# Layer two's contexts as whole blocks in six PSUM banks for blocks 0 to 12, with scale, offset and residual in slots of their own

## The chip, the cores and the metric

The kernel runs on one core of a Trainium2 chip. The metric is the device time in microseconds (us); the time before is the median of three runs. TensorE (PE) multiplies, VectorE (DVE), ScalarE (ACT) and GpSimd (POOL) work elementwise, and SyncE (SP) issues the DMAs.

## What is computed

`x` has 128 graphs of 64 nodes with 768 features, and each graph has a 64 x 64 adjacency. Everything is 32-bit floating point. Cut to what matters:

```python
h = jnp.maximum(_layernorm(x, axis=-1), 0.0)
for l in range(2):
    m_left  = jnp.einsum('bsh,oh->bso', h, W_left[l])
    m_right = jnp.einsum('bsh,oh->bso', h, W_right[l])
    u_left  = jnp.einsum('bih,bjh->bij', h, m_left) / temper
    u_right = jnp.einsum('bih,bjh->bij', h, m_right) / temper
    u = u_left * adj_tri + u_left * diag_mask + u_right * jnp.swapaxes(adj_tri, 1, 2)
    delta_exp_u = jnp.exp(u) * adj
    attention = delta_exp_u / (jnp.sum(delta_exp_u, axis=2, keepdims=True) + 1e-10)
    h_lin = jnp.einsum('bsh,oh->bso', h, W_lin[l]) + b_lin[l]
    ctx = jnp.matmul(attention, h_lin)
    h = jax.nn.relu(_layer_norm(ctx, ln_a[l], ln_b[l]))
return x + h
```

`_layer_norm` subtracts the mean over the 768 features, divides by the standard deviation (with `ddof=1`) plus 1e-3, multiplies by `ln_a` and adds `ln_b`. For layer two the last lines become: scale each row of the context by one number and by the row `a`, add the row `b` (the offset), take the maximum with zero and add `x` (the residual).

## The kernel before

The 8192 tokens are cut into 16 blocks (`NB`) of 512 tokens, that is 8 graphs. Each layer has two passes over them. `pass_one` makes the scores and the attention and stores it in DRAM. `pass_two` makes `h_lin` and the context of each block and finishes its rows. The change lies in layer two's `pass_two`, where `last` is true.

**The projection.** `linear(u, ...)` makes `h_lin` of block `u` from 15 products (`ORDER`), numbered 0 to 14: sums of token chunks times sums of weight chunks. The products go to four PSUM banks, X, Z, Y and V, in the order X Z X Y X V X Y X V X Y V Z V. After each product `read` adds the bank into the tile `hl`: the first time that a part of `hl` is written by ScalarE (`L305`), later ones by VectorE (`L223`). Four times per block a bank is begun anew with a bias in it: `fresh` lets ScalarE copy it there (`L843`, "preload") ahead of the product. The preload of V for product 9 is issued after product 6; it has to wait until the V of product 5 has been read.

**The token sums.** Eleven of the products use sums of token chunks (`T_SUMS`), made by GpSimd (`L223`, tile `ts`) a block ahead, from slot 15 on. Ahead of them ScalarE applies layer one's affine and relu to the loaded tokens (`affine`, `L382`, six parts from slot 9).

**Slots.** The order of the work on each engine is that of issue. `put(slot, f)` files a function; `linear` runs slot `2*i` in the middle of product `i`, after its first two matmul calls, and slot `2*i+1` after the product and its reads. What is filed at 30 or later is moved to the next block (30 becomes 0). Every engine's queue is in order, so a slot is a place in the queues and not a time: an instruction that waits holds what is queued behind it on its engine.

**The context in two halves.** A block has four tiles of 128 rows, numbered (r, k). `finish(u, r)` calls `context` for the two tiles of half `r`: 8 calls of 64 x 64 tiles on 384 columns into four banks (`aux0`, `aux1`). ScalarE squares both tiles with a sum along the row and takes the root (`L1022`, `L1024`), VectorE makes the inverse (`L1027`, `L1028`). For layer two, `scaled` then lets VectorE multiply each tile by its inverse and by `a` in one instruction (`L1032`) and GpSimd add `b` (`L1035`, the offset). `done` lets VectorE take the maximum with zero and add `x` in one instruction (`L1046`, the residual), and SP store the rows (`L1048`). `residual` loads `x` into the tiles `xr` (`L962`), of which there are four. In layer two every block `u - 1` is finished so within `linear(u)`: half 0 after product 0, half 1 after product 7, with slots 6, 7, 8, 11, 12 and 20, 21, 22, 30, 30 for inverse, two scalings and two residuals.

**The context in one.** Layer one's blocks 0 to 12 are finished by `finish_block(u - 1)` after product 12 of `linear(u)`. `context_block` makes all four tiles in one group of 16 calls, on 512 and 256 columns, into six banks: those of `aux0` and `aux1` used more tightly, and X and Y of the projection. VectorE copies the parts in X and Y to SBUF (`L972`), after which X gets its preload for the next block. ScalarE squares eight pieces (`squares`, `L983`, slots 25, 26, 28, 29); the deviation and inverse follow in slots 30 and 32, and the scaling of the pieces in slots 33 to 36. In layer one this scaling is ScalarE's (`L997`), with no `a`, offset or residual: layer two applies those to the tokens as it loads them.

Of the kernel before, what the change touches and what calls it, by code (L numbers as in the profile page):

```python
# [13 lines left out]
ALU = mybir.AluOpType  # L14
# [3 lines left out]
def kernel(  # L18
# [12 lines left out]
    nc = tc.nc  # L31
# [33 lines left out]
    def put(slot, *fs):  # L65
        plan.setdefault(slot, []).extend(fs)
# [780 lines left out]
    def pass_two(l, aside):  # L847
        last = l == L - 1
        with (tc.tile_pool(name=f"ps_two{l}", bufs=1, space=bass.MemoryType.PSUM) as ps,
# [108 lines left out]
            def residual(u, r):  # L958
                XS[u, r] = [sp.tile([P, H], F32, name="xr", bufs=4) for _ in range(2)]
                for k in range(2):  # L960
                    for h in range(PAIR):
                        nc.sync.dma_start(XS[u, r][k][h * S:(h + 1) * S], x[u * NBB + batch(r, k, h)])  # L962

            def finish_block(u, more):

                parts = context_block(u)
                tiles = ((0, 0), (0, 1), (1, 0), (1, 1))
                zs = {t: sp.tile([P, H], F32, name="z", bufs=4) for t in tiles}
                cut = (slice(0, T), slice(T, H))

                for t in ((1, 1), (1, 0)):
                    nc.vector.tensor_copy(zs[t][:, cut[0]], parts[t][0])  # L972
                    parts[t][0] = zs[t][:, cut[0]]
                    if t == (1, 1):
                        AHEAD.append(fresh(l, 0, more))
                ss = stat.tile([P, Q, 2], F32, name="ssb", bufs=2)
                sd = stat.tile([P, Q], F32, name="sdb", bufs=2)
                rs = stat.tile([P, Q], F32, name="rsb", bufs=2)

                def squares(t):  # L980
                    junk = zs[0, t[1]]
                    for n in range(2):
                        nc.scalar.activation(junk[:, cut[n]], parts[t][n], AF.Square,  # L983
                                             accum_out=ss[:, 2 * t[0] + t[1], n:n + 1])

                def deviation():
                    nc.vector.reduce_sum(sd, ss, axis=mybir.AxisListType.X)
                    nc.scalar.activation(sd, sd, AF.Sqrt, bias=floor, scale=1.0 / (H - 1.0))

                def inverse():  # L990
                    nc.vector.tensor_scalar_add(rs, sd, EPS_LN)
                    nc.vector.reciprocal(rs, rs)

                def scaled(t):
                    by = rs[:, 2 * t[0] + t[1]:2 * t[0] + t[1] + 1]
                    for n in range(2):
                        nc.scalar.activation(zs[t][:, cut[n]], parts[t][n], AF.Copy, scale=by)  # L997
                    kept(u, *t, zs[t])

                order = ((1, 1), (1, 0), (0, 0), (0, 1))  # L1000
                for f, slots in ((squares, (25, 26, 28, 29)), (scaled, (33, 34, 35, 36))):
                    for n, t in zip(slots, order):
                        put(n, lambda f=f, t=t: f(t))
                put(30, deviation)
                put(32, inverse)

            def kept(u, r, k, z):
                for h in range(PAIR):
# [2 lines left out]
            def finish(u, r):  # L1011

                cx = context(u, r)
                zs = [sp.tile([P, H], F32, name="z", bufs=4) for _ in range(2)]
                if last and not u and not r:
                    residual(u, r)
                two = "p (n d) -> p n d"
                ss = stat.tile([P, 2], F32, name="ss", bufs=2)
                sd = stat.tile([P, 2], F32, name="sd1", bufs=2)
                rs = stat.tile([P, 2], F32, name="rs1", bufs=2)  # L1020
                for k in range(2):
                    nc.scalar.activation(zs[k].rearrange(two, n=2), cx[k], AF.Square, accum_out=ss[:, k:k + 1])  # L1022

                nc.scalar.activation(sd, ss, AF.Sqrt, bias=floor, scale=1.0 / (H - 1.0))  # L1024

                def inverse():
                    nc.vector.tensor_scalar_add(rs, sd, EPS_LN)  # L1027
                    nc.vector.reciprocal(rs, rs)  # L1028

                def scaled(k):  # L1030
                    if last:
                        nc.vector.scalar_tensor_tensor(  # L1032
                            zs[k].rearrange(two, n=2), cx[k], rs[:, k:k + 1],
                            rows["a"].rearrange(two, n=2), op0=ALU.mult, op1=ALU.mult)
                        nc.gpsimd.tensor_add(zs[k], zs[k], rows["b"])  # L1035
                        return
                    if (u, r, k) == (NB - 1, 1, 1):
                        nc.vector.tensor_scalar_mul(zs[k].rearrange(two, n=2), cx[k], rs[:, k:k + 1])
                    else:
                        nc.scalar.activation(zs[k].rearrange(two, n=2), cx[k], AF.Copy, scale=rs[:, k:k + 1])  # L1040
                    kept(u, r, k, zs[k])

                def done(k):
                    if last:
                        xs = XS[u, r]
                        nc.vector.scalar_tensor_tensor(xs[k], zs[k], 0.0, xs[k], op0=ALU.max, op1=ALU.add)  # L1046
                        for h in range(PAIR):
                            nc.sync.dma_start(out[u * NBB + batch(r, k, h)], xs[k][h * S:(h + 1) * S])  # L1048
                        if k and u + r < NB - 1 and (u, r) != (NB - 2, 0):
                            residual(u + r, 1 - r)  # L1050

                steps = [lambda f=f, k=k: f(k) for f in (scaled, done) for k in range(2)]
                return [inverse] + (steps if last else steps[:2])

# [37 lines left out]
            for u in range(NB):  # L1092
                turn = not last and u >= NB - 2
                put(4, lambda u=u: load_at(u))
                if u + 1 < NB:
                    if u:
                        load_h(2, l, u + 1)
                        put_all(9, affine(2, l, u + 1))
                    put_sums_t((2, l, u + 1), 15 if u else 21, 1, 0)
                    if not last and NB - 5 <= u < NB - 3:  # L1100
                        load_rows(1, u + 5 - NB, sp)
                        put_all(14, transpose_rows(1, u + 5 - NB, sp), 2)
                    if not last and u >= NB - 3:
                        put(2, lambda u=u: load_h(1, 1, u + 3 - NB))
                        put_all(21 if u == NB - 3 else 11, affine(1, 1, u + 3 - NB), 1 if u == NB - 3 else 3)
                    if u in aside:
                        aside[u]()
                    ends = {}
                    if u and last:
                        ends = {0: ((u - 1, 0), (6, 7, 8, 11, 12)), 7: ((u - 1, 1), (20, 21, 22, 30, 30))}  # L1110
                    elif u > NB - 3:
                        ends = {5: ((u - 1, 0), (16, 17, 18)), 11: ((u - 1, 1), (28, 29, 30))}
                    elif u:
                        ends = {12: (u - 1, None)}
                    linear(u, (0, 1), 0, ends, (0, 1) if u + 2 < NB else (0,))
                    for n in sorted(plan):
                        plan[n - 30] = plan.pop(n)
                else:
                    if turn:
                        put_token_ops(1, 0, "before")  # L1120
                        assert not idle, len(idle)
                        for n in range(RINGS - 1):
                            put(20 + 4 * n, lambda n=n: stream(1, n))
                        ends = ({1: ((u - 1, 0), (13, 14, 16)), 11: ((u - 1, 1), (34, 35, 36))},
                                {4: ((u, 0), (50, 51, 52))})
                    else:
                        last_block(u)
                        put(8, lambda: residual(u - 1, 1))
                        ends = ({0: ((u - 1, 0), (12, 13, 15, 19, 31)), 9: ((u - 1, 1), (28, 29, 30, 39, 41))},
                                {2: ((u, 0), (44, 48, 51, 61, 62))})  # L1130
                    linear(u, (0,), 0, ends[0], (1,))
                    linear(u, (1,), 30, ends[1], ())
                    for n in sorted(plan):
                        run(n)
                    for f in (finish_last if last else finish)(u, 1):
                        f()
# [72 lines left out]
```

## Time and profile before

| what | value |
|---|---|
| median of three runs | 2706.51 us (2705.50 to 2709.24) |
| profiled execution: own time, span | 2705.84 us, 2704.1 us |
| granted TensorE clock | 0.998 |
| busy: PE, DVE, ACT, POOL | 2677.7, 1499.1, 832.4, 1381.4 us |
| layer one's second pass, whole blocks | about 941 to 1304 us of the span |
| layer two's second pass | about 2226 us to the end |
| VectorE scaling `L1032` | 62 of 1.01 us |
| GpSimd offset `L1035` | 62, 1.82 us median |
| VectorE residual `L1046` on `xr` | 60, 2.02 us median, 0.95 to 2.44 |

A line of the profile names engine, code line, operation, tiles (written `out<-in`), shapes, a count and durations. "L1046" is line 1046 of the kernel. Several instructions of one kind in a row are merged on the timeline: the first number is the start and the second the time until the last one ends. In brackets stands how long the engine was idle before, and what released it. The product names are those of the banks, so "V" is a product, or a read, in bank V.

### The profile page before, as it was taken

Reading aid. Unit: us, or ns where it says so; the run is one execution under the profiler, and the core shown is the slowest. Engines: PE = TensorE matmul, PEld = TensorE weight load, DVE = VectorE, ACT = ScalarE, POOL = GpSimd, SP = SyncE. Lnnn points to the kernel's source line nnn. Section 1 sums busy time; section 2 is a strip of 40 time slices with the busy share of each in tenths; the row PEclk is TensorE's granted clock in tenths of the full one; section 3 lists DMA queues with packets and bytes.
Section 4 is the critical chain, followed back from the end, with each engine's and each line's share of the span. In section 5 each row is a group of like instructions: output and inputs, shape, how many; then the busy total and the mean of one; then the engine's idle time right before and its main releaser. Section 6 shows DMA issues by size and latency. Waiting matters only on the chain.

```text
span 2704.1 us, 47306 instructions
## 1 busy us (share of the span) xinstructions
PE 2677.7 (99%) x18514; PEld 2301.3 (85%) x18514; DVE 1499.1 (55%) x2456; ACT 832.4 (31%) x1617; POOL 1381.4 (51%) x1071
## 2 busy tenths in 40 slices
PE   9999999999999999999999999999999999999998
PEld 8788888888888888888788888888888888888886
DVE  7664755756647433334344545546446475666667
ACT  4032131221310254454631221221212304445443
POOL 6633244333336765566433325335244286887886
PEclk9999999999999999999999999999999999999999
DMA  8886956858765345558594956968759524655655
GB/s 272 268 309 212 289 197 208 279 202 265 244 207 181 102 143 184 166 167 255 184 284 174 317 187 212 286 191 279 229 193 301 211 79 135 182 160 159 186 154 148
DMA packets 310222, 567.81 MB, mean 210 GB/s; under 512 B 62832, under 2 KB 190064, under 8 KB 301808
## 3 DMA queue, kind: packets, MB, share of 16 engines
q1 hardware_dynamic: 309840, 564.39, 64.9%
q8 instruction: 148, 2.42, 0.4%
q14 instruction: 74, 0.61, 0.1%
q10 hardware_dynamic: 160, 0.39, 0.0%
HBM read 429.40 MB, written 135.27 MB: 209 GB/s over the span
## 4 chain that ended last, share of the span: by engine, by line
PE 96%; DVE 1%; SPq 0%; issue 0%; DMA 0%; ACT 0%; DVEq 0%; ACTq 0%
PE right L535 17%; PE X L1069 12%; PE X L535 11%; PE V L535 11%; PE Z L535 9%; PE Y L535 9%; PE V L1069 8%; PE Y L1069 6%; PE both L474 5%; PE Z L1069 4%; PE aux L877 2%; PE aux L900 1%; PE Y L900 0%; PE Z L474 0%; DVE wp L223 0%
## 5 line engine op out<-in xcount | busy, mean ns | idle before, releaser
L223 POOL TENSOR_TENSOR ts<-ht 128x512 f32<-128x512 f32 x352 | 481.6, 1374 | 172.6 <-PE X L1069 69.6
L223 POOL TENSOR_TENSOR ts<-ht,ts 128x512 f32<-128x512 f32 x192 | 252.9, 1324 | 345.7 <-PE V L535 202.1
L535 PE MATMUL right<-ts,wp 128*128 128x252 f32 (+1 forms) x1632 | 380.9, 376 | 0.6 <-DVE wp L223 0.6
L535 PEld LDWEIGHTS right<-ts,wp 128*128 128x128 f32 x1632 | 310.0, 190 | 39.5 <-DVE wp L223 1.0
L483 POOL TENSOR_TENSOR wm<-adj,tri 128x256 f32<-128x256 f32 x60 | 42.3, 728 | 490.7 <-DMA wp<-ws 274.5
L223 DVE TENSOR_TENSOR m<-m,X 128x512 f32<-128x512 f32 x160 | 105.5, 684 | 257.9 <-ACT m L305 180.2
L223 DVE TENSOR_TENSOR m<-m,right 128x504 f32<-128x504 f32 (+1 forms) x304 | 199.5, 674 | 87.8 <-PE right L535 74.1
L1069 PE MATMUL X<-room,ts 128*128 128x256 f32 x1024 | 244.0, 380 | 0.2
L535 PE MATMUL Z<-ts,wp 128*128 128x256 f32 x992 | 234.3, 379 | 0.0
L223 POOL TENSOR_TENSOR ts<-ht,ht 128x512 f32<-128x512 f32 x128 | 163.2, 1285 | 137.8 <-PE right L535 92.8
L1069 PEld LDWEIGHTS X<-room,ts 128*128 128x128 f32 x1024 | 191.7, 190 | 31.7 <-issue 1.8
L535 PEld LDWEIGHTS Z<-ts,wp 128*128 128x128 f32 x992 | 188.4, 190 | 24.9
L535 PE MATMUL X<-ts,wp 128*128 128x256 f32 x872 | 207.5, 381 | 1.9 <-DVE wp L223 1.9
L535 PE MATMUL V<-ts,wp 128*128 128x252 f32 (+1 forms) x864 | 201.6, 376 | 0.0
L305 ACT ACTIVATE m<-right 128x504 f32<-128x504 f32 (+1 forms) x64 | 36.2, 592 | 506.8 <-PE both L474 486.8
L535 PEld LDWEIGHTS X<-ts,wp 128*128 128x128 f32 x872 | 164.4, 190 | 25.5 <-POOL ts L223 2.3
L382 ACT ACTIVATE ht<-ht,b_col,a_col 128x512 f32<-128x512 f32 x192 | 141.3, 806 | 140.9 <-DMA ht<-h 140.9
L1069 PE MATMUL Y<-room,ts 128*128 128x256 f32 x768 | 182.5, 379 | 0.0
L535 PEld LDWEIGHTS V<-ts,wp 128*128 128x128 f32 x864 | 164.2, 190 | 20.4
L1069 PEld LDWEIGHTS Y<-room,ts 128*128 128x128 f32 x768 | 145.8, 190 | 20.4 <-issue 0.6
L223 DVE TENSOR_TENSOR hl<-hl,V 128x512 f32<-128x512 f32 (+1 forms) x136 | 89.2, 656 | 128.9 <-PE V L1069 118.7
L223 DVE TENSOR_TENSOR m<-m,Y 128x512 f32<-128x512 f32 x144 | 95.8, 684 | 116.0 <-PE Y L535 105.2
(225 smaller groups left out, 4866.3 us busy)
## 6 DMA issues: line engine op xcount, KB each, us to landing
wp<-ws SPq DMA_DIRECT2D x435, 512.0 KB, 6.3
ht<-h SPq DMA_DIRECT2D x62, 1536.0 KB, 8.3
h<-room SPq DMA_DIRECT2D x112, 384.0 KB, 7.1
z<-z SPq DMA_DIRECT2D x128, 192.0 KB, 3.1
ws<-wp SPq DMA_DIRECT2D x93, 256.0 KB, 4.2
xr<-in_x_dram SPq DMA_DIRECT2D x120, 192.0 KB, 3.6
out_dram<-xr SPq DMA_DIRECT2D x120, 192.0 KB, 2.6
room<-z SPq DMA_DIRECT2D x112, 192.0 KB, 5.1
```

The costliest lines, as they stand in the source:

```text
L223: (eng.tensor_add if sign == "+" else eng.tensor_sub)(o, a, b)
L305: nc.scalar.activation(to(o), p, AF.Copy, scale=1.0 if sign == "+" else -1.0)
L382: nc.scalar.activation(ht, ht, AF.Relu, bias=cols[1][:, c:c + 1], scale=cols[0][:, c:c + 1])
L474: nc.tensor.matmul(p[h * S + e:h * S + e + 32, q, e:e + 95], ht[:, c, b * S + e:b * S + e + 32], mb[:, e:e + 95], start=(c == 0), stop=(c ...
L483: nc.gpsimd.tensor_tensor(wm[:, :, k], adj[:, :, 1 - k], tri[:, k].unsqueeze(1).to_broadcast([P, Q, S]), op=ALU.mult)
L535: nc.tensor.matmul(p[:, g], wk[:, c, g * P:(g + 1) * P], tk[:, c, :].rearrange("p (b s) -> p b s", s=S)[:, :, :ns], start=(new and g == c ...
L877: nc.tensor.matmul(cx[k][i, m, :HH], at[j, q, :], hl[j, q, m * HH:(m + 1) * HH], start=True, stop=True)
L900: nc.tensor.matmul(parts[r, k][n][i], at[j, q, :], hl[j, q, cut], start=True, stop=True)
L1069: nc.tensor.matmul(p[:, n], b[t][:, c, r * P:(r + 1) * P], w[s][:, c, :], start=(i in FIRST and i not in PRELOAD and n == c == 0), stop=(c ...
```

## The change

- In layer two, blocks 0 to 12 go through `finish_block` as in layer one. The copy of tile (1, 0) out of Y is then ScalarE's instead of VectorE's.
- The scaling is done in place of `L1032` by two VectorE instructions per tile, one for each piece; the offset stays GpSimd's. Both are in slots 33 to 36, so 3 to 6 of the block after.
- The residual has slots 38 to 41, so 8 to 11, for the tiles (1,1), (1,0), (0,0) and (0,1); it is moved to a function, `added_rows`.
- The `x` rows of a block are loaded in slot 12, all eight loads together, those of block 0 in slot 20 of `linear(0)`.
- The last three blocks keep their halves; the halves of block 13 now follow products 6 and 11 of `linear(14)`, and those of block 14 products 2 and 10 of `linear(15)`, with later slots.

```diff
--- before.py
+++ after.py
@@ -969,7 +969,7 @@
                 cut = (slice(0, T), slice(T, H))
 
                 for t in ((1, 1), (1, 0)):
-                    nc.vector.tensor_copy(zs[t][:, cut[0]], parts[t][0])
+                    (nc.scalar.copy if last and t == (1, 0) else nc.vector.tensor_copy)(zs[t][:, cut[0]], parts[t][0])
                     parts[t][0] = zs[t][:, cut[0]]
                     if t == (1, 1):
                         AHEAD.append(fresh(l, 0, more))
@@ -993,17 +993,34 @@
 
                 def scaled(t):
                     by = rs[:, 2 * t[0] + t[1]:2 * t[0] + t[1] + 1]
+                    if last:
+                        for n in range(2):
+                            nc.vector.scalar_tensor_tensor(zs[t][:, cut[n]], parts[t][n], by, rows["a"][:, cut[n]],
+                                                           op0=ALU.mult, op1=ALU.mult)
+                        nc.gpsimd.tensor_add(zs[t], zs[t], rows["b"])
+                        return
                     for n in range(2):
                         nc.scalar.activation(zs[t][:, cut[n]], parts[t][n], AF.Copy, scale=by)
                     kept(u, *t, zs[t])
 
                 order = ((1, 1), (1, 0), (0, 0), (0, 1))
-                for f, slots in ((squares, (25, 26, 28, 29)), (scaled, (33, 34, 35, 36))):
+                steps = [(squares, (25, 26, 28, 29)), (scaled, (33, 34, 35, 36))]
+                if last:
+                    steps.append((lambda t: added_rows(u, *t, zs[t]), (38, 39, 40, 41)))
+                    for r in range(2):
+                        put(42, lambda r=r: residual(u + 1, r))
+                for f, slots in steps:
                     for n, t in zip(slots, order):
                         put(n, lambda f=f, t=t: f(t))
                 put(30, deviation)
                 put(32, inverse)
 
+            def added_rows(u, r, k, z):
+                xs = XS[u, r][k]
+                nc.vector.scalar_tensor_tensor(xs, z, 0.0, xs, op0=ALU.max, op1=ALU.add)
+                for h in range(PAIR):
+                    nc.sync.dma_start(out[u * NBB + batch(r, k, h)], xs[h * S:(h + 1) * S])
+
             def kept(u, r, k, z):
                 for h in range(PAIR):
                     nc.sync.dma_start(ROWS[u][batch(r, k, h)], z[h * S:(h + 1) * S])
@@ -1012,8 +1029,6 @@
 
                 cx = context(u, r)
                 zs = [sp.tile([P, H], F32, name="z", bufs=4) for _ in range(2)]
-                if last and not u and not r:
-                    residual(u, r)
                 two = "p (n d) -> p n d"
                 ss = stat.tile([P, 2], F32, name="ss", bufs=2)
                 sd = stat.tile([P, 2], F32, name="sd1", bufs=2)
@@ -1042,12 +1057,9 @@
 
                 def done(k):
                     if last:
-                        xs = XS[u, r]
-                        nc.vector.scalar_tensor_tensor(xs[k], zs[k], 0.0, xs[k], op0=ALU.max, op1=ALU.add)
-                        for h in range(PAIR):
-                            nc.sync.dma_start(out[u * NBB + batch(r, k, h)], xs[k][h * S:(h + 1) * S])
-                        if k and u + r < NB - 1 and (u, r) != (NB - 2, 0):
-                            residual(u + r, 1 - r)
+                        added_rows(u, r, k, zs[k])
+                        if k and (u, r) == (NB - 3, 1):
+                            residual(NB - 2, 0)
 
                 steps = [lambda f=f, k=k: f(k) for f in (scaled, done) for k in range(2)]
                 return [inverse] + (steps if last else steps[:2])
@@ -1106,8 +1118,11 @@
                     if u in aside:
                         aside[u]()
                     ends = {}
-                    if u and last:
-                        ends = {0: ((u - 1, 0), (6, 7, 8, 11, 12)), 7: ((u - 1, 1), (20, 21, 22, 30, 30))}
+                    if last and not u:
+                        for r in range(2):
+                            put(20, lambda r=r: residual(0, r))
+                    if last and u > NB - 3:
+                        ends = {6: ((u - 1, 0), (18, 19, 20, 23, 24)), 11: ((u - 1, 1), (28, 29, 30, 33, 34))}
                     elif u > NB - 3:
                         ends = {5: ((u - 1, 0), (16, 17, 18)), 11: ((u - 1, 1), (28, 29, 30))}
                     elif u:
@@ -1126,7 +1141,7 @@
                     else:
                         last_block(u)
                         put(8, lambda: residual(u - 1, 1))
-                        ends = ({0: ((u - 1, 0), (12, 13, 15, 19, 31)), 9: ((u - 1, 1), (28, 29, 30, 39, 41))},
+                        ends = ({2: ((u - 1, 0), (14, 15, 17, 21, 31)), 10: ((u - 1, 1), (29, 30, 31, 39, 41))},
                                 {2: ((u, 0), (44, 48, 51, 61, 62))})
                     linear(u, (0,), 0, ends[0], (1,))
                     linear(u, (1,), 30, ends[1], ())
```

## The prediction

> **What bounds the kernel now.** I read the page first (shares and chain), then the busy table of the steady stretches of both second passes, then the timelines of one block each. All times are of the one profiled execution.
>
> ```profile
> PE 2677.7 (99%) x18514; PEld 2301.3 (85%) x18514; DVE 1499.1 (55%) x2456; ACT 832.4 (31%) x1617; POOL 1381.4 (51%) x1071
> ...
> PE 96%; DVE 1%; SPq 0%; issue 0%; DMA 0%; ACT 0%; DVEq 0%; ACTq 0%
> ```
>
> TensorE is the bound and has no slack. A microsecond gained elsewhere is worth nothing; a wait put in front of a matmul is paid in full. Layer one's second pass already uses six banks for whole blocks, so its blocks price the new form. One block of each layer, in the busy table of the two stretches:
>
> ```profile
> core 0: us, PE busy (x) PEld busy (x) DVE busy (x) ACT busy (x) POOL busy (x), PEclk, DMA share, GB/s
> 1001.37:1030.21 28.84, 28.84 (x153) 23.75 (x153) 10.82 (x17) 13.49 (x36) 18.78 (x16) 1.00 0.48 160
> 2341.50:2370.70 29.20, 29.20 (x153) 23.60 (x153) 19.86 (x25) 13.68 (x26) 23.64 (x16) 1.00 0.57 167
> ```
>
> Layer one repeats every 28.84 us and layer two every 29.20 us, both with TensorE full. The fifteen projections cost the same (1.727 us each); what differs is the contexts, 2.94 us in one group against 3.30 in two. But layer two has 9 us more VectorE work and 5 us more GpSimd work per block, the part that the change rearranges. The next views show what those do to each other, first before (VectorE, then GpSimd):
>
> ```profile
> 2350.43 0.69 DVE L223 TENSOR_TENSOR hl<-hl,V 128x512 f32<-128x512 f32 x1 [0.91 <-PE V L1069]
> 2351.04 3.99 DVE L1046 SCALAR_TENSOR_TENSOR xr<-z,xr 128x768 f32<-128x768 f32 x2
> 2357.26 1.28 DVE L223 TENSOR_TENSOR hl<-hl,X 128x512 f32<-128x512 f32 x2 [2.23 <-PE X L1069]
> ...
> 2348.68 3.60 POOL L1035 TENSOR_TENSOR z<-z,b 128x768 f32<-128x768 f32 x2 [3.78 <-DVE z L1032]
> 2352.23 3.93 POOL L223 TENSOR_TENSOR ts<-ht 128x512 f32<-128x512 f32 x2
> 2356.24 1.27 POOL L223 TENSOR_TENSOR ts<-ts,ht 128x512 f32<-128x512 f32 x1
> ```
>
> The residual instruction (L1046, both inputs in SBUF) takes 2.0 us here and 0.95 where GpSimd is idle (the two at 2691.4). GpSimd's sum takes 1.97 beside it and 1.27 alone. Read one by one, the first L1046 ends 0.82 us after the offset addition L1035 ends, and the next sum can only then begin: the two engines take turns. So in steady overlap a residual costs 0.82 behind whatever GpSimd holds, and GpSimd waits for it. Today two residuals form a batch and sit after the V read (the first line), so the delay reaches no matmul.
>
> **What the Trainium skill says.** "SBUF — State Buffer", section "Who interferes with whom": a VectorE instruction with two SBUF inputs contends with a GpSimd instruction that reads SBUF, and one with at most one SBUF input does not. The trace agrees: L1046 is slowed to 2.02 (median), L1032 with its PSUM input stays at 1.01 in all 62 cases. Section "SBUF: two separate sides": whichever starts first has the port for its whole instruction; the trace's turns agree. "TensorE: Matmul & The Clock Gate", section "Why this matters for your kernels", warns of idle gaps over about 3 us; the granted clock here is 1.00 and no such gap occurs in these stretches, so no run here shows it. I take no clock loss for gaps of 2 us.
>
> **The change part by part.** I set 0 at the start of product 0 of a block. The layer-one timeline gives TensorE's places (block from 1004.86):
>
> ```profile
> 1013.49 1.89 PE L1069 MATMUL V<-room,ht 128*128 128x256 f32 x8
> ...
> 1018.67 1.89 PE L1069 MATMUL X<-room,ht 128*128 128x256 f32 x8
> 1020.40 1.89 PE L1069 MATMUL V<-room,ht 128*128 128x256 f32 x8
> 1022.12 1.89 PE L1069 MATMUL X<-room,ts 128*128 128x256 f32 x8
> ...
> 1017.64 0.59 ACT L843 COPY V<-bias 128x512 f32<-128x512 f32 x1
> ```
>
> Product 5 (V) ends at 10.4; product 9 starts bank V anew at 15.54, and needs before it VectorE's read of product 5 (0.69) and ScalarE's preload (0.59). So that read must start by about 14.2. Product 10 writes X at 17.26, and needs VectorE's two reads of product 8 (1.28), which must start by 15.9.
>
> *Contexts.* Two groups become one: 3.30 − 2.94 = 0.36 us of TensorE saved in each of 13 blocks, −4.6 us. The banks X and Y are asked for at 22.5; their last reads are done by about 21.6 in layer one, and the preload of X for the next block ends 3.8 us before its use (1029.87 against 1033.7). Both hold here: nothing else of VectorE lies there. The copy moved to ScalarE (0.6) delays the squares, which end near 0.6 instead of 0.06, and their reduction waits anyway for V's read at 0.8. ScalarE's next read is due at 1.9. Eight square pieces replace four, about as in layer one; hidden. No cost, unless VectorE is late there.
>
> *Scaling, slots 3 to 6.* Eight pieces instead of four whole rows. VectorE gets to them after the Z read, at 4.9 (layer one: 1009.75). By width from 0.87 a piece-pitch for 768 in SBUF, 0.92 from PSUM, 0.61 and 0.34 for 512 and 256 reads: each tile 0.95, together 3.8. So they end at 8.7, and the Y read of product 3 runs to 9.3 (Y is written at 12.1; no loss).
>
> *Offset, same slots.* Four L1035 of 1.77 pitch on GpSimd, queued one after the other instead of two and two. The first becomes ready at 6.0, but the SBUF half of the second tile's scaling holds the port to 6.5. It runs 6.5–8.3, the second 8.3–10.0.
>
> *Residual, slots 8 to 11.* Three of the four now stand in VectorE's queue ahead of product 5's V read. They take turns with the offsets: residual 1 waits to 10.0, ends 10.9; offset 3 to 12.6; residual 2 to 13.4; offset 4 to 15.2; residual 3 to 16.0. V's read runs 16.0–16.6, the preload to 17.25, and product 9 starts at about 17.3: **1.8 us late**. The fourth residual then waits for the first transform sum (1.2 us of port) and ends at 18.05. The X reads of product 8 end at 19.3, and product 10, now free from 19.0, waits another 0.3. Sum: **2.0 us per block**. ScalarE stands behind the preload too (two affine parts and Y's read of product 7), but these are done by 19.3, ahead of the Y product at 21.
>
> The rest of the block is in time: the sums start at 16 and end at 30.7 of a 30.8 us block (11 × 1.27), each ahead of its use.
>
> *DMAs.* Per block still 8 stores, 8 residual loads, one token load and one attention load, all on SP. The stores follow the residuals to 18.6; the loads at slot 12 wait for those stores to land (2.6 to 3.4 us) and go out from about 19 to 25 (0.6 each); then the next token load, landing (8.3 us) some 3 into the next block, where the affine parts want it at 8.6. No cost; if SP were 5 us later, the affine parts would be late next.
>
> *Count.* The stall comes in blocks 2 to 13 in full: 12 × 2.0 = 24.0. In block 14 half a context stands ahead of product 9 (1.64 us), so little is left; its squares wait for z tiles, its residual loads land about 25 into it: +0.7 for this and the moved ends of block 15, bounds −1 and +3. Block 0's loads at slot 20 and the last two blocks' other halves are neutral. Total: −4.6 + 24.0 + 0.7 = +20.1; I take **+20**. Against the profiled execution (span 2704.1, own time 2705.84) that is 2725.9; against the median 2706.51, 0.7 above it, **2726.5**.
>
> Not shown by the trace: who wins the port when both wait, with four offsets in a row. If GpSimd always does, as in the 13 repetitions seen, the stall is 2.0 (1.5 to 2.4 for errors in the start and the piece widths). If the port cost nothing at all, the offsets would end at 7.8, 9.6, 11.3 and 13.1, residual 3 at 12.2, the V read would be in time and the stall 0. These are the two ends.
>
> **Rivals.**
>
> *A, the turns with the offsets delay the V read:* +20, own range +13 to +26.
>
> *B, VectorE sometimes wins twice:* residuals 1 and 2 go together at 10.0, residual 3 follows offset 3 at 13.4, the V read is in time at 14.2–14.9, and only the fourth residual, behind offset 4, holds the X reads (to 18.2, 0.9 late). 12 × 0.9 − 4.6 + 0.7 = +7, 2713. Against it: no L1046 in the trace goes ahead of a waiting GpSimd instruction.
>
> *C, no stall:* the V read starts before 14.2, because the offsets begin or proceed faster than I queue them; it decides there. Then only the contexts count: −4.6, 2701.9, not slower. For it: VectorE has 9 us free per block, and layer one runs this form at 28.84. Against it: layer one's scaling is on ScalarE and has no offset or residual.
>
> *D, a longer chain:* the fourth residual or late loads push the reads of products 10 and 11 too, or delay the token load; another 1 to 2 us per block, +32 to +44. Against it: the margins above.
>
> That the change does nothing for TensorE is not likely: the same function gives 28.84 in layer one.
>
> **Chances and range.** A 0.65, B 0.12, C 0.15, D 0.08. A measurement of this kernel tells about 0.2% (5.4 us) from no change. A and D are slower, B mostly (0.09); C, at 0.17%, is mostly within (0.11), and 0.04 of it beyond. So slower 0.82, same 0.14, faster 0.04. The range from 2708 to 2742 holds A, most of B and the near part of D; it leaves out C.
>
> **What would show it.** Right: TensorE idle once per block in layer two ahead of product 9's V (about 1.8 us, behind ScalarE's preload, itself behind VectorE), and a trace of it ahead of product 10; a block of about 30.8 us; offsets of 1.8 alternating with residuals of over 2 us; contexts in one group of 2.9 us with X and Y in time. Wrong: blocks of 28.84 with TensorE full (C), or the gap ahead of product 10 alone (B), or a gap ahead of the contexts or of products 0 to 4, which my queue does not have.

## The result, and the profile after

The changed kernel takes 2732.36 us (median of 4 runs, 2732.07 to 2733.55) against 2707.77 before on the same chip (median of 4 as well): ratio 1.0092, 95% interval [1.0077, 1.0107]. It is 0.9% slower. The forecast was 2726.5 within 2708 to 2742. The profiled execution has a span of 2730.5 us against 2704.1.

The page first: TensorE's share and the chain of waits.

```profile
PE 2680.8 (98%) x18514; PEld 2303.6 (84%) x18514; DVE 1509.5 (55%) x2508; ACT 842.9 (31%) x1721; POOL 1386.4 (51%) x1071
...
PE 89%; DVE 6%; issue 1%; DMA 1%; ACT 1%; SPq 0%; POOL 0%; DVEq 0%; ACTq 0%
```

No engine's total moved by more than 11 us, and yet the chain, which was TensorE's for 96%, now runs through VectorE for 6%. The work is the same; some of it has come onto the path. The busy table of a steady block of layer two, from product 0 to the next product 0, shows how much:

```profile
core 0: us, PE busy (x) PEld busy (x) DVE busy (x) ACT busy (x) POOL busy (x), PEclk, DMA share, GB/s
2342.49:2373.31 30.82, 29.30 (x153) 23.68 (x152) 20.64 (x28) 14.55 (x36) 24.07 (x15) 1.00 0.54 154
```

Such a block takes 30.81 us on average instead of 29.20, and for 1.5 us of it TensorE is idle at the full granted clock. The next lines are the timelines of that block: TensorE, VectorE, GpSimd, and ScalarE.

```profile
2359.72 1.99 PE L1081 MATMUL V<-room,ht 128*128 128x256 f32 x8 [1.52 <-ACT V L843]
2361.64 1.99 PE L1081 MATMUL X<-room,ts 128*128 128x256 f32 x8
...
2352.19 6.25 DVE L1020 SCALAR_TENSOR_TENSOR xr<-z,xr 128x768 f32<-128x768 f32 x3
2358.36 0.68 DVE L223 TENSOR_TENSOR hl<-hl,V 128x512 f32<-128x512 f32 x1
2358.96 1.42 DVE L1020 SCALAR_TENSOR_TENSOR xr<-z,xr 128x768 f32<-128x768 f32 x1
2360.31 1.27 DVE L223 TENSOR_TENSOR hl<-hl,X 128x512 f32<-128x512 f32 x2
...
2348.60 9.03 POOL L1000 TENSOR_TENSOR z<-z,b 128x768 f32<-128x768 f32 x4 [6.58 <-DVE z L998]
2357.58 3.94 POOL L223 TENSOR_TENSOR ts<-ht 128x512 f32<-128x512 f32 x2
...
2359.07 0.59 ACT L843 COPY V<-bias 128x512 f32<-128x512 f32 x1 [3.70 <-DVE hl L223]
```

Read it backwards. Product 9 (V, 2359.72) waits for ScalarE's preload of V; the preload waits 3.7 us for VectorE's read of product 5's V; that read could have begun when product 5 ended, at about 2353.0, but it stands in VectorE's queue behind three residuals (L1020), which take 6.25 us instead of 2.7; and beside them lie four offsets (L1000), 9.03 us instead of 7.1. Read one by one, the second to fourth offset end at 2352.64, 2355.14 and 2357.62, and the residuals at 2353.46, 2355.95 and 2358.44, each 0.82 us after an offset: the two engines take turns. Product 10 follows 1.92 us after product 9 and not 1.73: the X reads end at 2361.58, 0.06 before it. The table of waits over blocks 2 to 13 has the wait of product 9 as the one long wait of TensorE (in all 18.1 us, 12 times, the longest 1.5):

```profile
PE V L1081 <- ACT V L843: 18.1, 12, 1.5
```

The chain also has 1% for DMA: in this block a store lands just as the third residual begins. It isn't the cause: the run "no offset" below has the same stores, and there this residual starts right behind the second and takes 0.95 us.

### The profile page after: what moved, and what is told of

It is laid out like the page before. It is cut to its first block, busy times and chain, and to the rows that moved or that the text cites. A ratio compares the mean times of both kernels' runs of the same rounds, so it can differ in the third digit from the quotient of the medians.

```text
span 2730.5 us, 47378 instructions
## 1 busy us (share of the span) xinstructions
PE 2680.8 (98%) x18514; PEld 2303.6 (84%) x18514; DVE 1509.5 (55%) x2508; ACT 842.9 (31%) x1721; POOL 1386.4 (51%) x1071
## 4 chain that ended last, share of the span: by engine, by line
PE 89%; DVE 6%; issue 1%; DMA 1%; ACT 1%; SPq 0%; POOL 0%; DVEq 0%; ACTq 0%
PE right L535 17%; PE X L535 11%; PE V L535 11%; PE X L1081 9%; PE Z L535 9%; PE Y L535 9%; PE V L1081 7%; PE both L474 5%; PE Y L1081 5%; PE Z L1081 4%; DVE xr L1020 2%; PE aux L900 2%; DVE z L998 2%; DVE hl L223 1%; PE Y L900 1%
## 5 line engine op out<-in xcount | busy, mean ns | idle before, releaser
L223 POOL TENSOR_TENSOR ts<-ht 128x512 f32<-128x512 f32 x352 | 470.2, 1343 | 184.8 <-PE X L1081 89.2
L223 POOL TENSOR_TENSOR ts<-ht,ts 128x512 f32<-128x512 f32 x192 | 243.5, 1275 | 342.9 <-PE V L535 200.3
L1000 POOL TENSOR_TENSOR z<-z,b 128x768 f32<-128x768 f32 x52 | 117.2, 2285 | 87.8 <-DVE z L998 87.8
```

What stands on the lines that cost most here:

```text
L223: (eng.tensor_add if sign == "+" else eng.tensor_sub)(o, a, b)
L1000: nc.gpsimd.tensor_add(zs[t], zs[t], rows["b"])
```

## The experiments

The parts of the kernel ahead of layer two's second pass are the same in all kernels, but in the single profiled executions that pass starts anywhere from 2224.9 to 2232.0 us. So beside the measured time I give the length of the second pass itself, from the start of its second product (ahead of which TensorE still waits 0.57 us for the weights) to the end of TensorE's last matmul.

| kernel | second pass, us | median time, us | ratio to before, 95% interval |
|---|---|---|---|
| before | 466.7 | | |
| the change | 492.0 | 2732.36 | 1.0092 [1.0077, 1.0107] |
| two residuals ahead | 468.7 | 2708.99 | 1.0007 [0.9998, 1.0015] |
| all residuals behind | 521.8 | 2762.00 | 1.0201 [1.0186, 1.0216] |
| offset set aside | 494.8 | 2733.00 | 1.0092 [1.0075, 1.0109] |
| no offset | 466.9 | 2705.44 | 0.9994 [0.9986, 1.0003] |
| copy back on VectorE | 492.0 | 2730.61 | 1.0090 [1.0071, 1.0108] |
| early turn, first try | 467.3 | 2708.04 | 1.0006 [0.9999, 1.0012] |
| early turn at block 11 | 463.5 | 2702.82 | 0.9988 [0.9981, 0.9994] |
| early turn at block 12 | 463.9 | 2703.70 | 0.9991 [0.9984, 0.9998] |

The median before was 2707.77 us beside the change, 2707.14 beside the next four rows, 2707.15 beside "copy back" and the first early turn, and 2706.08 beside the last two.

**Offset set aside.** Is it the port, or do the residuals only wait for the data of their offsets? (The line that makes room for the tile is left out here.)

```diff
-                        nc.gpsimd.tensor_add(zs[t], zs[t], rows["b"])
+                        nc.gpsimd.tensor_add(rows["s"], zs[t], rows["b"])   # a tile that nobody reads
```

> In the whole blocks of layer two GpSimd's offset reads the scaled tile as before but writes a tile that nobody reads, so b is left out of the rows of blocks 0 to 12 and no residual has to wait for an offset's data. Port turns (theory): the port is taken as before, so nothing changes: blocks of 30.8 us, 2730 to 2734. Rival, the residuals wait for the data of their offsets (four of 1.8 us one after the other): they now run one after the other from 9.4 us, V's read is in time, blocks of 28.84: about 2709 or less.

Measured 2733.00, the time of the change. VectorE and GpSimd in the same place of a block:

```profile
2351.29 6.34 DVE L1022 SCALAR_TENSOR_TENSOR xr<-z,xr 128x768 f32<-128x768 f32 x3
2357.56 0.68 DVE L223 TENSOR_TENSOR hl<-hl,V 128x512 f32<-128x512 f32 x1
...
2347.71 9.12 POOL L1002 TENSOR_TENSOR s<-z,b 128x768 f32<-128x768 f32 x4 [6.58 <-DVE z L1000]
```

No residual needs anything of an offset here, and the three still take 6.34 us and the offsets 9.12; blocks are 30.92 us. One by one, the residuals end at 2352.67, 2355.15 and 2357.64, each again 0.82 us after an offset. The wait for data is out as the cause of the stall in the whole blocks. What is shown is that the two engines' instructions exclude each other in time; that it is the shared port of SBUF which does it is what the Trainium skill states ("SBUF — State Buffer", section "Who interferes with whom").

Its second pass is 2.8 us longer than the change's: 0.1 in each of the 12 blocks, and 1.5 in the last two, where the clock fell for a while (last section).

**No offset.** The same line left out.

> In the whole blocks of layer two the offset is left out, so b is not added to the rows of blocks 0 to 12 and GpSimd does nothing from about 0 to 10 us of a block. Both the port turns and the wait for the offsets' data are gone: residuals of about 0.9 us, V's read in time, blocks of 28.84 us: 2705 to 2709 (the last blocks may gain a little too). Rival, the splitting of the scaling into eight pieces or the whole-block contexts themselves hold TensorE in layer two: the gap ahead of product 9 stays, about 2732.

Measured 2705.44; blocks of 28.84, layer one's figure to the hundredth.

```profile
2347.76 2.69 DVE L1019 SCALAR_TENSOR_TENSOR xr<-z,xr 128x768 f32<-128x768 f32 x3
2350.37 0.68 DVE L223 TENSOR_TENSOR hl<-hl,V 128x512 f32<-128x512 f32 x1
```

Three residuals in 2.69 us, 0.90 each. So the eight pieces of the scaling and the contexts in six banks make TensorE wait no more in layer two than in layer one. The last blocks, which keep their offsets, still have two waits (0.94 and 1.88 us): a part of the loss does not come from the whole blocks.

**Two residuals ahead.** The theory gives a place for each residual: two can end before V has to be read, a third between that and the X reads of product 8, the fourth behind these. The edit in short:

```diff
-(38, 39, 40, 41) ... put(42, lambda r=r: residual(u + 1, r))
+(38, 39, 41, 47) ... put(48, lambda r=r: residual(u + 1, r))   # blocks 0 to 11; block 12 as in the change
```

> Blocks 0 to 11 put two residuals ahead of the V read of product 5, one behind it, and the fourth behind the X reads of product 8 (slots 38, 39, 41, 47 in place of 38 to 41), with the loads of x in slot 48; block 12 and the last three are as in the changed kernel. Port turns (theory): the second residual ends at 13.3 us of the block, V's read is in time (by 14.2), the third residual ends at 15.9 and the X reads at 17.1, just in time (17.26). Blocks of 28.84 to 29.1 us instead of 30.81, in 12 blocks: 20 to 24 us off, so 2709 to 2712. Rival, VectorE simply has too much to do in whole blocks: the same work in other places stalls as before, about 2732.

Measured 2708.99, blocks of 28.87. VectorE, and below it TensorE's products 9 and 10:

```profile
2375.65 3.76 DVE L1021 SCALAR_TENSOR_TENSOR xr<-z,xr 128x768 f32<-128x768 f32 x2
2379.33 0.68 DVE L223 TENSOR_TENSOR hl<-hl,V 128x512 f32<-128x512 f32 x1
2379.92 1.97 DVE L1021 SCALAR_TENSOR_TENSOR xr<-z,xr 128x768 f32<-128x768 f32 x1
2381.82 1.27 DVE L223 TENSOR_TENSOR hl<-hl,X 128x512 f32<-128x512 f32 x2
...
2381.49 1.89 PE L1082 MATMUL V<-room,ht 128*128 128x256 f32 x8
2383.22 1.92 PE L1082 MATMUL X<-room,ts 128*128 128x256 f32 x8
```

The same instructions, as slow as before (3.76 for two, 1.97 for one), but the V read ends 1.5 us ahead of product 9, and the X reads 0.13 ahead of product 10. The gap is gone in all 12 blocks, 23 us of second pass. So it was neither VectorE's total nor the turns as such, but the turns in front of a read that TensorE waits for.

**All residuals behind.** The opposite test: nothing ahead of the V read (in short again).

```diff
+(41, 42, 43, 44) ... put(45, lambda r=r: residual(u + 1, r))   # blocks 0 to 11
```

> Blocks 0 to 11 put all four residuals behind the V read of product 5 (slots 41 to 44), with the loads of x in slot 45. Port turns (theory): the gap ahead of product 9 goes, but the residuals now take turns with the last two offsets and the first two sums: they end at 12.7, 15.3, 17.3 and 19.4 us, and the X reads of product 8 at 20.6, so product 10 starts 3.4 us late. Blocks of about 32.3 us, 12 x 1.4 = 17 us more than the changed kernel: about 2749. Rival, only the place ahead of the V read matters (each residual costs about 0.9 on VectorE, which is free from there on): blocks of 28.84, about 2709.

Measured 2762.00: a wait in the right place and the wrong one in size. The gap left product 9 and stood ahead of product 10 in every block, but 9 of the 12 blocks took 33.7 us and 3 took 32.0, where 32.3 was expected. The busy table of a 32.0 and a 33.7 block, and of the first 3.3 or 3.4 us behind the gap, first in the 33.7 block and then in the 32.0 one:

```profile
2366.75:2398.80 32.05, 29.11 (x153) 23.76 (x152) 20.93 (x29) 14.42 (x34) 23.94 (x16) 1.00 0.53 153
2398.80:2432.50 33.70, 30.79 (x152) 24.90 (x152) 20.90 (x29) 14.43 (x34) 23.89 (x16) 0.95 0.50 144
2401.70:2405.00 3.30, 3.29 (x8) 2.61 (x9) 0.55 (x1) 0.00 (x0) 3.22 (x3) 0.55 0.96 255
...
2369.60:2373.00 3.40, 3.33 (x15) 2.96 (x16) 1.84 (x4) 0.00 (x0) 3.32 (x3) 1.00 0.96 256
```

The block of 32.0 is the queue's working. In the other one shown the granted clock (the number after POOL) was 0.55 behind the gap, and product 10's eight matmuls took 3.3 us instead of 1.7. In each of the nine it stood at a half for 3.41 us, begun 0.2 to 1.2 us into product 10, so each lost the same 1.7 us; the last section comes back to this. So the 12 x 1.4 expected were 12 x 1.2 of waits, and 9 x 1.7 of clock on top.

**Copy back on VectorE.** The first edit of the diff undone.

> The changed kernel with the copy of tile (1, 0) out of bank Y given back to VectorE. If that edit costs and brings nothing (the prediction's step): VectorE is idle there (product 13 is not read for another 3 us), blocks of 30.8 us, 2731 to 2734. Rival, the copy on VectorE would hold the squares, and through them the inverse and the scaling: blocks longer by about 0.5 us, 2738.

Measured 2730.61 (two executions, just below the expected 2731), second pass 492.0 in both. The copy is free on either engine.

**The turn from whole blocks to halves.** With two residuals ahead the second pass is still 2.0 us longer than before, though its 13 whole blocks save 4.3 us. The rest, 6.3 us, lies in blocks 14 and 15. TensorE and VectorE there, in the changed kernel:

```profile
2680.83 1.96 PE L1081 MATMUL V<-room,ts 128*128 128x256 f32 x8 [1.93 <-DVE hl L223]
...
2692.47 1.10 PE L1081 MATMUL Y<-room,ts 128*128 128x256 f32 x4 [1.88 <-DVE hl L223]
...
2675.60 4.49 DVE L1020 SCALAR_TENSOR_TENSOR xr<-z,xr 128x768 f32<-128x768 f32 x2 [0.21 <-POOL z L1050]
...
2687.94 4.05 DVE L1020 SCALAR_TENSOR_TENSOR xr<-z,xr 128x768 f32<-128x768 f32 x2 [2.24 <-POOL z L1050]
```

The first wait comes behind the residuals of block 13's first half, at slots 23 and 24 ahead of the V read of product 12; the second behind those of its second half, in the last block, whose products take half the time. Here the residuals do wait for data too: VectorE stood idle for 2.24 us until GpSimd, busy with token sums, had made the offset (L1050). From product to product the two waits cost 2.1 and 2.0 us (3.82 instead of 1.73, and 2.90 instead of 0.86). Another 1.1 us lies in the last block's context at 2704.10, which takes 2.55 us instead of 1.45 behind a late scaling, and the rest in products and contexts that are 0.1 to 0.3 us late. I made the turn two blocks earlier, so that blocks 13 and 14 could stand as before the change (cut to the slots of the two blocks of the turn; slots and loads of the whole blocks are those of "two residuals ahead", and the last two blocks have their old lines back):

```diff
+if last and u == NB - 4:
+    ends = {9: ((u - 1, 0), (21, 22, 23, 29, 29)), 14: ((u - 1, 1), (32, 33, 34, 41, 42))}
+elif last and u == NB - 3:
+    ends = {3: ((u - 1, 0), (9, 10, 10, 17, 19)), 8: ((u - 1, 1), (20, 21, 22, 30, 30))}
```

> The residual slots and loads of the run with two residuals ahead of the V read, for whole blocks 0 to 10; blocks 11 and 12 go in halves two blocks earlier than in the change (after products 9 and 14, then 3 and 8, with slots that keep the residuals off the reads of V, X and Y), so that blocks 13 and 14 stand again where they stood before the change. If the 6 us that the moved ends of blocks 13 and 14 cost are VectorE and GpSimd meeting in the shorter products of the last block (theory): they go, and there remain 11 x 0.36 us of contexts saved less 10 x 0.03: 3.6 us faster than before the change, 2702 to 2705. Rival, going from whole blocks to halves costs that wherever it is done: about 2709.

Measured 2708.04: a miss. The last two blocks are clean, but the two blocks of the turn have waits of 0.38, 1.87 and 1.14 us. TensorE, ScalarE and SP at the longest:

```profile
2617.28 1.99 PE L1083 MATMUL X<-room,ht 128*128 128x256 f32 x8 [1.87 <-ACT hl L305]
...
2613.82 2.93 ACT L382 ACTIVATE ht<-ht,b_col,a_col 128x512 f32<-128x512 f32 x4 [2.96 <-DMA ht<-h]
...
2600.87 3.05 SPq L1022 DMA_DIRECT2D out_dram<-xr  x4
2604.17 3.02 SPq L962 DMA_DIRECT2D xr<-in_x_dram  x4
2607.28 0.53 SPq L375 DMA_DIRECT2D ht<-h  x1
```

The token load (L375) stands in SP's queue behind stores that wait for their residuals, and loads that wait for these stores. It comes late, ScalarE's affine parts wait for it, and the X read behind them. The next two runs mend that by one slot (30 in place of 29 puts the residuals behind the load), and the two waits for V by moving scalings and residuals off the V reads (the new slots alone):

```diff
+9: ((u - 1, 0), (20, 21, 21, 30, 30)), 14: ((u - 1, 1), (32, 33, 34, 38, 39))
+3: ((u - 1, 0), (9, 11, 11, 17, 17)), 8: ((u - 1, 1), (20, 21, 22, 30, 30))
```

> As the run with the early turn (whole blocks 0 to 10, blocks 13 and 14 as before the change), with two places mended that its trace shows: the residuals of block 11's first half go to slot 30, so behind the load of the next tokens in SP's queue and not ahead of it (that load came late, and with it ScalarE's affine parts and a read of X: 1.9 us), and the scalings and residuals of blocks 11 and 12 are moved off the reads of bank V that products 14 waited for (0.4 and 1.1 us). If these three waits are what the turn costs (theory): second pass of layer two 3.4 to 3.6 us shorter than before the change, 2703 to 2704.5. Rival, the turn from whole blocks to halves makes new waits wherever it is done: about 2707.

> The same one block later: whole blocks 0 to 11, halves of block 12 in the block of the turn, those of block 13 in the one after it, block 14 as before the change. Theory: 0.3 us better than the run that turns at 11, if the last block's shorter products meet nothing late; rival, VectorE and GpSimd come late into the last block as in the change, 2705 to 2709.

Measured 2702.82 and 2703.70, second passes of 463.5 and 463.9. With the turn at 11 the token load goes out ahead of the stores:

```profile
2600.08 0.52 SPq L375 DMA_DIRECT2D ht<-h  x1
2603.48 3.13 SPq L1022 DMA_DIRECT2D out_dram<-xr  x4
```

No wait of TensorE behind the pass's second product is then longer than 0.11 us. The ratio to before is 0.9988 [0.9981, 0.9994]: a little faster than the kernel before. The second pass is 3.2 us shorter, where 3.4 to 3.6 were expected; eleven contexts in one group save 4.0, and the rest goes on small delays. The slots were moved together, so what each move brought is not shown. The turn at 12 brings one more whole block and a new wait of 0.53 us in the last one, so the 0.3 us hoped for did not come; the two runs can't be told apart.

## Why the prediction was right or wrong

- **What bounds, and the contexts' saving: right.** A block without waits in layer two took 28.84 (no offset), as layer one's; 0.36 us per block was there to be had.
- **The stall's place and size: right.** With 0 at product 0 (2342.49) the forecast and the trace are: second offset ends 10.0 and 10.15; residuals 10.9, 13.4, 16.0 and 10.97, 13.46, 15.95; V read 16.6 and 16.55; product 9 at 17.3 and 17.23; product 10 at 19.3 and 19.15. The forecast of 2.0 us per block was 1.97. Rival B is out: in every whole block a GpSimd instruction ended between any two residuals. C is out by the stall itself, and D because no other long wait of TensorE stands in these blocks.
- **One step was off and did no harm, by luck.** The scaling was priced at 0.95 us per tile, from reads of the same widths; its own pieces follow each other after 0.66 and 0.40 us, so it took 4.3 us and not 3.8. VectorE came to its residuals at 9.7 instead of 9.3, still ahead of the second offset's end at 10.15; so the first turn hid the error.
- **The last blocks: mis-sized.** The term "+0.7, bounds −1 and +3" was 6.3 us, outside its own bounds. I had looked at the x loads and z tiles, which did not hold TensorE, and not at where the moved residuals stand against the reads of V and Y; the working done for product 9 was not done for them. The total still lies within rival A's own +13 to +26, whose width came mostly from the stall (1.5 to 2.4 us per block) and not from this term; that is luck. The sum by second passes: −4.6 + 12 x 1.97 + 6.3 = +25.3, and 25.3 measured.
- **Costed at nothing, and so it was:** the copy on ScalarE (tested) and the squares (no wait of TensorE at products 0 to 4). No clock loss was taken for gaps of 2 us, and the changed kernel has none; but that was close, see the last section. The residual loads and the token load did no harm in the change; the first early turn shows that SP's margin is real but can be used up by one slot.
- **Base:** the spans of the two profiled executions differ by 26.4 us, 1.1 more than their second passes: 1.5 lie ahead of the pass, in parts that are equal, and 0.3 come off behind it.

## What to carry to other kernels

Before merging two groups of work into one, write down for each in-order queue which instruction has a deadline set by the bound engine, and count what the merge puts ahead of it, at the durations in company and not alone: here 3 x 0.9 us had become 6.25. VectorE's residuals, with two SBUF inputs, and GpSimd's offsets worked in turns here, so batches of them side by side cost the sum of both; then place, not amount, decides: the same instructions in slots 8, 9, 11 and 17 cost 0.03 us a block instead of 1.97. And price the turn between two schemes like the steady blocks: here it was worth more than the whole gain.

## What the runs showed of the hardware

- **Gaps and the clock.** With all residuals behind, the second pass has ten stretches in which the granted clock is a half, each 3.41 us long: nine behind the twelve gaps of 2.9 us, and one behind a gap of 1.93 in block 14. With the offset set aside, a gap of 1.89 us in the last block did the same, and the changed kernel's 1.88 at the same place did not:

```profile
2690.54:2693.95 3.41, 1.52 (x7) 1.06 (x6) 3.34 (x7) 0.77 (x3) 2.28 (x1) 1.00 0.57 148
2693.95:2697.36 3.41, 3.41 (x9) 2.69 (x8) 2.16 (x5) 0.38 (x1) 1.81 (x1) 0.50 0.90 242
...
2689.72:2693.13 3.41, 1.53 (x8) 1.06 (x7) 3.34 (x7) 0.76 (x2) 2.76 (x1) 1.00 0.44 112
2693.13:2696.55 3.42, 3.37 (x19) 2.38 (x21) 2.86 (x5) 0.39 (x1) 2.01 (x2) 1.00 0.86 237
```

The first pair is the offset set aside, the second the change; the first two numbers after the window are its length and TensorE's busy time (by the trace's modelled ends), and the clock stands after POOL. Within a trace, the stretches of half clock start a whole number of 3.41 us apart: with all residuals behind at 2303.05, then 10 times 3.41 later at 2337.18, 19 times later at 2402.03, and so on. (In the change, the grid is known from the half clock behind TensorE's last matmul, from 2723.85.) Cut into windows on that grid, every one of these eleven stretches follows a window in which TensorE was idle for 1.89 us or more. The three gaps of 2.9 us without one are cut by the grid so that no window holds more than 1.77, 1.86 and 1.92 of them; the two gaps of 1.9 without one, in the change, had at most 1.88 in one window. So in these traces it is the idle time within one window that counts, with the border at about 1.9 us, and not the length of the gap alone. The Trainium skill ("TensorE: Matmul & The Clock Gate", section "Why this matters for your kernels") warns of gaps over about 3 us; here shorter ones were enough.

- **Turns.** They were strict: with both engines waiting, each of a block's first three residuals ended 0.81 to 0.82 us after an offset and each offset 1.67 to 1.69 after a residual, in all 13 whole blocks, whether they shared data or not.
- **PSUM input.** VectorE pieces of the scaling with a PSUM input took 0.47 to 0.48 us at 256 and 0.74 at 512 columns, the same beside a busy GpSimd (the change) as without its offsets (no offset).
